# Attention of the small heads: score products by half row blocks, with ScalarE's order written out

## The chip, the core and the metric

The kernel runs on one core of one Trainium2 chip. The time is device microseconds (us) of one execution of the whole program, taken as the median of several runs. Five engines work beside each other, each through its own instructions in order: TensorE (PE in the profile; its weight loads are listed as PEld), VectorE (DVE), ScalarE (ACT), GpSimd (POOL) and SyncE (SP), which issues most of the DMA transfers. They wait for one another through semaphores. TensorE writes into PSUM, which has 8 banks; one bank holds 512 float32 numbers in each of 128 partitions.

## What is computed

The reference is a decoder of two layers over 16 sequences of 128 tokens with 256 features. Each layer has a self attention, a cross attention and a feed-forward part, each followed by a layer norm. The change is in the self attention of the second layer, which has 32 heads of 8 features each:

```python
def _sliding_window_attention(x, Wq, Wk, Wv, Wo, n_heads=32, window=128):
    B, T, D = x.shape                  # 16, 128, 256
    H, dk = (n_heads, D // n_heads)    # 32, 8
    bs = window
    nb = T // bs                       # 1
    ...
    scores = jnp.einsum('bhnrd,bhncd->bhnrc', qb, kw) * scale
    ...
    valid = (dist >= 0) & (dist <= window) & (key_global >= 0)
    scores = jnp.where(valid[None, None], scores, jnp.finfo(scores.dtype).min)
    probs = jax.nn.softmax(scores, axis=-1)
    out = jnp.einsum('bhnrc,bhncd->bhnrd', probs, vw)
    ...
    return out @ Wo.T
...
x = _layernorm(x + _L1_attn_ref(x, L1_attn_Wq, L1_attn_Wk, L1_attn_Wv, L1_attn_Wo), axis=-1)
```

With 128 tokens and a window of 128 each token attends to itself and to all tokens ahead of it in its own sequence, so that the mask is a plain causal one and every sequence stands alone.

## The kernel before

**The stages.** The program is one long body: the three parts of layer 0, then the self attention of layer 1 (the stage of the change, 1695 to 1963 us of the profile), the cross attention of layer 1 (to about 2198 us), and a mixture of experts. A planner decides the order of the instructions of each engine from costs of its own and from the order of the source. Inside `with tc.manual_schedule(engines={mybir.EngineType.PE})` TensorE's order is that of the source, and the planner orders the other engines around it.

**The unit of work.** The 2048 tokens are 16 row blocks of 128 tokens (`t`), one for each sequence. The 256 features of queries and keys, transposed, are two halves of 128 partitions (`c`), with 16 heads in each. Four neighbouring heads take up 32 partitions. `masked_keys` (L1230, on GpSimd) writes the keys four times side by side into `kz`, and in copy j keeps only the features of head j of each four, so that one product of 32 partitions of queries with 512 columns of `kz` gives the scores of four heads: 128 queries by 4 x 128 keys, one PSUM bank. A half (`t`, `c`) has four such products.

**A step** of the loop is (`t`, `c`, `e`): half a half, two products, eight heads. `attend_scores` does this for a step:

- TensorE writes the causal mask into two PSUM banks by two products with the identity in bf16 (L1238), and adds two score products (L1242) with 32 rows each, on two different row strips of its array. `sc` has two buffers of two banks.
- VectorE takes the maximum of each row and head (`amx`, L1251) and subtracts it (`pr`, L1253); ScalarE takes the exponent (L1254). `pr` has three buffers.

`attend_transpose` turns `pr` around by eight transposes (L1262), four into each of the two `tp` banks, and ScalarE copies each bank to `prT` (L1263). `attend_context` works on a half, that is on two steps: 16 products with the values and 16 with ones (L1272), four of them at a time on four column strips, which gives the weighted sums and the sums of the weights, in `o2`. `attend_divide` (L1282, L1284, VectorE) divides the one by the other and leaves `oT`. `attend_output` (L1301) multiplies both halves of a row block by the output weights, and VectorE adds the result to the residual `xs[t]` (L1302). `norm` (L110 to L116) is the layer norm of four row blocks, with a logarithm and an exponent on ScalarE (L102, L103); `norm_T` (L126, L127) transposes its result.

**The order of the source in a step n:** the scores of step n; the context of the half that ended at step n-3; the transposes of step n-2; and one further piece of work that depends on n: `project_a` (queries or keys of a later group of four row blocks, L1356 and L1360 on ScalarE, in row blocks 0 to 11), `values_a` (L1365, and L1367 on ScalarE), `norm_T`, or `attend_output` of the row block before. All of these share one PSUM bank, `misc`.

The PSUM banks of the stage: four for `sc`, two for `tp`, one for `misc`, one for `o2`.

The cross attention of layer 1 calls `attend_scores` too, with one product of 64 rows in each bank and no mask.

Of the kernel before, what the change touches and what calls it, by code (L numbers as in the profile page):

```python
# [18 lines left out]
F32 = mybir.dt.float32  # L19
# [8 lines left out]
P = 128  # L28
HID = 256
NB = 16  # L30
NT = NB * P
NG = 4
# [16 lines left out]
def decoder(ctx: ExitStack, tc: tile.TileContext, w: dict, out: bass.AP):  # L49
    nc = tc.nc  # L50
# [1179 lines left out]
        nc.gpsimd.tensor_tensor(kz, bc(kT, 1, 4), bc(own, 2, P), ALU.mult)  # L1230
        return kz

    def attend_scores(wk, psum, qT, kz, blocks, mask):

        sc = psum.tile([P, 2, 4, P], F32, tag="sc", name="sc", bufs=2)
        if mask is not None:
            for b in range(2):
                nc.tensor.matmul(  # L1238
                    sc[:, b].rearrange("p j k -> p (j k)"), lhsT=ident16, rhs=mask, start=True, stop=False
                )  # L1240
        for b, r in enumerate(blocks):
            nc.tensor.matmul(  # L1242
                sc[:, b].rearrange("p j k -> p (j k)"),
                lhsT=qT[r],
                rhs=kz[r].rearrange("p j k -> p (j k)"),
                start=mask is None,
                stop=True,
            )
        sc = sc.rearrange("p b j k -> p (b j) k")
        mx = stat.tile([P, 8], F32, tag="amx", name="amx")  # L1250
        nc.vector.tensor_reduce(mx, sc, AX.X, ALU.max)  # L1251
        pr = wk.tile([P, 8, P], F32, tag="pr", name="pr", bufs=3)
        nc.vector.tensor_tensor(pr, sc, bc(mx, 2, P), ALU.subtract)  # L1253
        nc.scalar.activation(pr, pr, AF.Exp)  # L1254
        return pr
# [69 lines left out]
    def cross_tables():  # L1325
        cross_w["own"] = own_rows(xpool, 64, "own2")
        cross_w["ones"] = places(xpool, D2, "ones2")

        gain = cross_w["rows"][0][1]
        nc.vector.tensor_scalar_mul(gain, gain, 0.25)  # L1330

    with ExitStack() as ph:
        pool = ph.enter_context(tc.tile_pool(name="l1a", bufs=1))
        wk = ph.enter_context(tc.tile_pool(name="l1a_k", bufs=2))
        ps = ph.enter_context(tc.tile_pool(name="l1a_ps", bufs=1, space=PSUM))
        D1 = 8
        wqk = [load_w(pool, f"L1_attn_{nm}T") for nm in ("Wq", "Wk")]
        wv = load_w(pool, "L1_attn_WvT")
        wz = attend_weights(pool, "L1_attn_WoT", D1)
        own1 = own_rows(pool, 32, "own1")  # L1340
        ones1 = places(pool, D1, "ones1")
        causal = pool.tile([P, 4, P], BF16, name="causal")
        nc.gpsimd.memset(causal, 0.0)
        nc.gpsimd.affine_select(
            out=causal, in_=causal, compare_op=ALU.is_ge, fill=NEG, base=0, pattern=[[0, 4], [-1, P]], channel_multiplier=1
        )
        o2 = ps.tile([P, 2, 2, P], F32, name="o2")
        cross_load()
        moe_load()
        vs, qkT = {}, {}  # L1350

        def project_a(g, n, c):

            pp = ps.tile([P, G], F32, tag="misc", name="proj")
            for k in range(2):
                nc.tensor.matmul(  # L1356
                    pp, lhsT=wqk[n][:, k, c * P : (c + 1) * P], rhs=xT[g][:, k, :], start=k == 0, stop=k == 1
                )
            t = qkT[g, n, c] = wk.tile([P, G], F32, tag=f"qkT{n}{c}", name=f"qkT{n}{c}")
            nc.scalar.activation(t, pp, AF.Copy, scale=1.0 / math.sqrt(D1) if n == 0 else 1.0)  # L1360

        def values_a(t):
            pp = ps.tile([P, HID], F32, tag="misc", name="proj_v")
            for k in range(2):
                nc.tensor.matmul(pp, lhsT=xTt(t, k), rhs=wv[:, k, :], start=k == 0, stop=k == 1)  # L1365
            v = wk.tile([P, HID], F32, tag="v", name="v")
            nc.scalar.copy(v, pp)  # L1367
            vs[t] = wk.tile([P, HID // D1, 4, D1], F32, tag="vz", name="vz", bufs=3)
            placed(v, ones1, D1, vs[t])

        steps = [(t, c, e) for t in range(NB) for c in range(2) for e in range(2)]
        kzs, prs, prTs, oTs = {}, {}, {}, {}
        with tc.manual_schedule(engines={mybir.EngineType.PE}):
            for n in range(2):
                for c in range(2):
                    project_a(0, n, c)
            values_a(0)
            for n in range(len(steps) + 16):
                if n == 4:
                    cross_tables()  # L1380

                if n in (5, 7):
                    q = NB // 2 - 2 + n // 7
                    norm_pair_xT(q, norm_pair_T(q, ps, "misc"))
                if n < len(steps):
                    t, c, e = steps[n]
                    cols = slice((t % 4) * P, (t % 4 + 1) * P)
                    if e == 0:
                        kzs[c] = masked_keys(wk, qkT[t // 4, 1, c][:, cols], own1)
                    blocks = [slice(32 * i, 32 * i + 32) for i in (2 * e, 2 * e + 1)]  # L1390
                    prs[n] = attend_scores(
                        wk, ps, qkT[t // 4, 0, c][:, cols], kzs[c], blocks, causal.rearrange("p j k -> p (j k)")
                    )
                if 0 <= n - 3 < len(steps):
                    t, c, e = steps[n - 3]
                    if e == 1:
                        attend_context([prTs.pop(n - 4), prTs.pop(n - 3)], vs[t], ones1, o2[:, c], 16 * c)
                        oTs[t, c] = attend_divide(wk, o2[:, c])
                if 0 <= n - 2 < len(steps):
                    prTs[n - 2] = attend_transpose(wk, ps, prs.pop(n - 2))  # L1400
                t, r = n // 4, n % 4
                if r == 0 and t // 4 + 1 < NG:
                    project_a(t // 4 + 1, t % 4 // 2, t % 2)
                elif r == 1 and t + 1 < NB:
                    values_a(t + 1)
                elif r == 3 and 0 <= t - 1 < NB:
                    attend_output(ps, t - 1, [oTs.pop((t - 1, c)) for c in range(2)], wz)
                    if t % 4 == 0:
                        norm(t // 4 - 1)
                elif r == 2 and t // 4 >= 1 and t % 4 in (1, 2):  # L1410
                    norm_T(t // 4 - 1, t % 4 - 1, ps, "misc")

# [1 line left out]
    with ExitStack() as ph:  # L1416
# [51 lines left out]
        with tc.manual_schedule(engines={mybir.EngineType.PE}):  # L1468
# [8 lines left out]
            for n in range(len(steps) + 14):  # L1477
                if n < len(steps):
                    t, c = steps[n]
                    if c == 0 and t + 2 < NB:  # L1480
                        load_ctx(t + 2)
                    blocks = [slice(64 * b, 64 * b + 64) for b in range(2)]
                    prs[n] = attend_scores(wk, ps, cols[t, 0][:, c, :], kzs.pop((t, c)), blocks, None)

                t, r = n // 2, n % 2
                if r == 0 and t + 2 < NB:
# [142 lines left out]
```

## Time and profile before

| | us |
|---|---|
| median of 3 runs | 2725.06 (2724.89 to 2730.54) |
| the profiled execution, its own time | 2732.66 |
| its span in the profile | 2730.9 |
| TensorE busy over the span | 2518.5 (92%) |
| VectorE busy over the span | 1902.3 (70%) |
| ScalarE busy over the span | 1473.7 (54%) |
| stage of the change, first score product to first score product of the next stage | 1695.48 to 1985.64 |

The page of the profile has the busy time of each engine; groups of instructions by source line with the mean time of one; and the chain of work that ended last. The trace can be asked for more: the busy times in a stretch, who waited for whom, and the timeline, in which each line has the start, the time taken, the engine, the source line, the operation, output <- inputs, the shapes, how many instructions the line merges (xN), and in brackets the idle time of the engine ahead of it with what ended it. A float32 product appears as two records (x2 for each), a transpose as one.

From the first score product of one row block to that of the next it took, for row blocks 0 to 14: 10.99, 19.05, 17.27, 17.28, 17.27, 17.71, 17.70, 17.28, 17.27, 17.71, 17.70, 17.28, 15.56, 15.99 and 15.99 us. Those of 17.70 hold a `norm_T`, those from row block 12 on hold no `project_a`.

### The profile page before, as it was taken

To read this page: it belongs to the slowest core of one execution; us is meant where nothing else is said; L and a number is where in the kernel's file an instruction comes from. 1 tells how busy PE (TensorE), PEld (TensorE's weight loads), DVE (VectorE), ACT (ScalarE), POOL (GpSimd) and SP (SyncE) were. 2 spreads that over 40 slices of the span, in tenths; PEclk is the share of its full clock that TensorE was granted. 3 is DMA by queue.
4 is the path that set the end of the run, shared out by engine and by line. 5 is a ranking of instruction groups with operands and counts; after the bars stand their busy time and mean duration, and the time that the engine had idled before them with its cause. 6 is when DMAs were issued, how large, how long until landed. Compare 5 with 4: busy or idle time off the path is not lost. (4 is left out here: it accounts for less than half of the span.)

```text
span 2730.9 us, 39531 instructions
## 1 busy us (share of the span) xinstructions
PE 2518.5 (92%) x13877; PEld 1493.5 (55%) x13908; DVE 1902.3 (70%) x4353; ACT 1473.7 (54%) x2778; POOL 1215.0 (44%) x1336
## 2 busy tenths in 40 slices
PE   6999999999986789988998888999988899999998
PEld 3677777777764133433433335666655546564746
DVE  5677777877757999999999963777777742324232
ACT  3455555555543888887887872555554531313120
POOL 5644544444436888888888873233132200000000
PEclk9999999999998899999999999999999999999999
DMA  7000000000011555655665562100100021111120
GB/s 226 1 1 1 1 1 1 1 1 1 1 50 29 106 116 111 128 122 107 119 125 110 113 136 97 55 2 2 42 16 11 2 63 47 54 39 60 34 67 10
DMA packets 360182, 150.82 MB, mean 55 GB/s; under 512 B 294576, under 2 KB 341136, under 8 KB 359472
## 3 DMA queue, kind: packets, MB, share of 16 engines
q1 hardware_dynamic: 358592, 144.49, 22.8%
q0 software_dynamic: 1392, 3.81, 0.6%
q8 instruction: 110, 1.80, 0.3%
q14 instruction: 88, 0.72, 0.1%
HBM read 74.71 MB, written 2.23 MB: 28 GB/s over the span
## 5 line engine op out<-in xcount | busy, mean ns | idle before, releaser
L786 POOL CAST aT<-at 128x2048 bf16<-128x2048 uint8 x256 | 480.9, 1894 | 91.5 <-DMA at<-a 88.6
L774 ACT ACTIVATE a<-e,snl 128x2048 uint8<-128x2048 f32 x256 | 510.7, 1996 | 3.5
L753 DVE TENSOR_SCALAR_CACHE_REDUCE e<-s,qs,smx 128x1024 f32<-128x1024 f32 x256 | 335.0, 1334 | 16.9 <-PE s L746 15.9
L753 DVE TENSOR_SCALAR_CACHE_REDUCE e<-s,qs 128x1024 f32<-128x1024 f32 x256 | 319.8, 1280 | 36.7 <-PE s L746 31.2
L796 PE MATMUL o<-aT,vq 128*32 128x512 bf16 x1024 | 262.8, 391 | 3.1 <-POOL aT L786 3.1
L746 PE MATMUL s<-kT,qT 64*128 64x512 bf16 x1024 | 191.0, 397 | 31.8 <-DVE e L753 28.7
L1541 DVE TENSOR_TENSOR h<-h,up 128x512 f32<-128x512 f32 (+1 forms) x100 | 68.7, 687 | 193.1 <-PE up L1537 189.4
L1540 ACT ACTIVATE h<-gate 128x512 f32<-128x512 f32 (+1 forms) x100 | 59.7, 597 | 220.1 <-PE gate L1537 219.9
L796 PEld LDWEIGHTS <-vq 128*32 128x32 bf16 x1024 | 85.5, 98 | 163.6 <-issue 89.4
L1537 PE MATMUL gate<-xT,w_L_ffn_w1g 128*128 128x512 f32 x352 | 167.7, 595 | 0.0
L1537 PE MATMUL up<-xT,w_L_ffn_w1u 128*128 128x512 f32 x352 | 165.4, 592 | 0.0
L1251 DVE TENSOR_REDUCE amx<-sc 128x8 f32<-128x1024 f32 x96 | 116.7, 1216 | 64.9 <-PE sc L1242 64.7
L1568 PE MATMUL py<-w_L_ffn_w2T,h 128*128 128x256 f32 x704 | 154.6, 379 | 0.0
L1254 ACT ACTIVATE pr<-pr 128x1024 f32<-128x1024 f32 x96 | 101.6, 1059 | 88.3 <-DVE pr L1253 88.3
L1263 ACT COPY prT<-tp 128x512 f32<-128x512 f32 x192 | 104.3, 584 | 76.7 <-PE tp L1262 76.3
L868 PE MATMUL gu<-xT,wgu 128*128 128x256 f32 x448 | 135.4, 427 | 9.2 <-ACT xT L160 4.3
L1568 PEld LDWEIGHTS py<-w_L_ffn_w2T,h 128*128 128x128 f32 x704 | 133.7, 190 | 18.3
L408 ACT ACTIVATE pls<-sc,lm,rms_rs 128x128 f32<-128x128 f32 x256 | 113.8, 454 | 21.6 <-DVE lm L404 21.6
L338 PE MATMUL proj<-Wlk,xT 128*128 128x512 f32 x256 | 121.1, 595 | 3.2 <-DVE ck L306 1.2
L338 PE MATMUL proj<-Wq,xT 128*128 128x512 f32 x256 | 122.0, 599 | 0.9 <-DVE raw_Wlk L347 0.9
L465 PE MATMUL po<-Wo,mT 128*128 128x256 f32 x512 | 121.2, 380 | 1.4 <-ACT mT L457 1.4
L1253 DVE TENSOR_TENSOR pr<-sc,amx 128x1024 f32<-128x1024 f32 x96 | 117.0, 1219 | 5.7
(313 smaller groups left out, 5378.9 us busy)
## 6 DMA issues: line engine op xcount, KB each, us to landing
wgu<-in_L_ffn_gu SPq DMA_DIRECT2D x112, 128.0 KB
sh<-share SPq DMA_DIRECT2D x32, 256.0 KB
at<-a SPq DMA_TRANSPOSE x256
sh<-share SPq DMA_DIRECT2D x16, 224.0 KB
sh<-share SPq DMA_DIRECT2D x16, 192.0 KB
w_L_ffn_w1g<-in_L_ffn_w1g SPq DMA_DIRECT2D x1, 2816.0 KB
w_L_ffn_w1u<-in_L_ffn_w1u SPq DMA_DIRECT2D x1, 2816.0 KB
w_L_ffn_w2T<-in_L_ffn_w2T SPq DMA_DIRECT2D x1, 2816.0 KB
```

The source lines that it names most:

```text
L338: nc.tensor.matmul(pp.rearrange("p h d -> p (h d)"), lhsT=xTt(b, k), rhs=wts[nm, hg][:, k, :], start=k == 0, stop=k == 1)
L465: nc.tensor.matmul(outs[b], lhsT=st["mT"][:, h, :], rhs=wts["Wo", hg][:, h, :], start=hg == 0 and h == 0, stop=hg == 3 and h == 3,)
L746: nc.tensor.matmul(s[hh][:, c, :], lhsT=qT[t % 4][r, i, :], rhs=kT[r, i, at : at + G], start=True, stop=True)
L753: nc.vector.tensor_scalar(st["e"][hh][:, half, :], s[hh].rearrange("p a b -> p (a b)"), qs[2 * gp + u][:, 2 * i + hh : 2 * i + hh + 1], No ...
L774: nc.scalar.activation(a.bitcast(U8), st["e"][hh].rearrange("p a b -> p (a b)"), AF.Exp, bias=st["nm"][:, hh : hh + 1], accum_out=groups[g ...
L786: nc.gpsimd.tensor_copy(aT[:, :, hh, u * P : (u + 1) * P].rearrange("p (b j) q -> p b j q", j=2), st["at"][hh].bitcast(U8).rearrange("p b ...
L796: nc.tensor.matmul(o[r : r + 32].rearrange("p a b -> p (a b)"), lhsT=vq[:, n, 32 * i : 32 * i + 32], rhs=aT[:, n].rearrange("p a b -> p (a ...
L868: nc.tensor.matmul(ffn_ps[q][:, n, :], lhsT=wt[:, k, :], rhs=xT[q // 2][:, k, at], start=k == 0, stop=k == 1)
L1251: nc.vector.tensor_reduce(mx, sc, AX.X, ALU.max)
L1253: nc.vector.tensor_tensor(pr, sc, bc(mx, 2, P), ALU.subtract)
L1537: nc.tensor.matmul(pp[:rows], lhsT=wt[:, k, :], rhs=xT[g][:, k, :], start=k == 0, stop=k == 1)
L1568: nc.tensor.matmul(py, lhsT=h[:rows, i4 * P : (i4 + 1) * P], rhs=wt, start=n == 0, stop=n == len(parts) - 1)
```

## The change

The loop goes by halves (`t`, `c`) in place of steps. `attend_scores` now takes four row strips and both `sc` buffers at once: four mask products, then four score products on the four row strips, each into its own bank. What VectorE and ScalarE do with the scores is split off as `attend_exp`. `pr` has four buffers here and three in the cross attention, where nothing else changes.

The source order in a half h is: scores of half h; `project_a` or `norm_T`, if any; the context and division of half h-2; then for each of the two quarters e: maximum, subtraction and exponent of (h, e), and the transposes with their copies of (h-1, e); then `values_a`, or `attend_output` of the row block before and perhaps `norm`. ScalarE is now in the `manual_schedule` too, so that its instructions stand in this order: exponent of (h, 0), the two copies of (h-1, 0), exponent of (h, 1), the two copies of (h-1, 1). VectorE's and GpSimd's order is still the planner's.

```diff
@@ -1230,26 +1230,24 @@
         nc.gpsimd.tensor_tensor(kz, bc(kT, 1, 4), bc(own, 2, P), ALU.mult)
         return kz
 
-    def attend_scores(wk, psum, qT, kz, blocks, mask):
-
-        sc = psum.tile([P, 2, 4, P], F32, tag="sc", name="sc", bufs=2)
+    def attend_scores(psum, qT, kz, blocks, mask):
+
+        scs = [psum.tile([P, 2, 4, P], F32, tag="sc", name="sc", bufs=2) for _ in range(len(blocks) // 2)]
+        banks = [sc[:, b].rearrange("p j k -> p (j k)") for sc in scs for b in range(2)]
         if mask is not None:
-            for b in range(2):
-                nc.tensor.matmul(
-                    sc[:, b].rearrange("p j k -> p (j k)"), lhsT=ident16, rhs=mask, start=True, stop=False
-                )
-        for b, r in enumerate(blocks):
+            for bank in banks:
+                nc.tensor.matmul(bank, lhsT=ident16, rhs=mask, start=True, stop=False)
+        for bank, r in zip(banks, blocks):
             nc.tensor.matmul(
-                sc[:, b].rearrange("p j k -> p (j k)"),
-                lhsT=qT[r],
-                rhs=kz[r].rearrange("p j k -> p (j k)"),
-                start=mask is None,
-                stop=True,
+                bank, lhsT=qT[r], rhs=kz[r].rearrange("p j k -> p (j k)"), start=mask is None, stop=True
             )
-        sc = sc.rearrange("p b j k -> p (b j) k")
+        return [sc.rearrange("p b j k -> p (b j) k") for sc in scs]
+
+    def attend_exp(wk, sc, bufs):
+
         mx = stat.tile([P, 8], F32, tag="amx", name="amx")
         nc.vector.tensor_reduce(mx, sc, AX.X, ALU.max)
-        pr = wk.tile([P, 8, P], F32, tag="pr", name="pr", bufs=3)
+        pr = wk.tile([P, 8, P], F32, tag="pr", name="pr", bufs=bufs)
         nc.vector.tensor_tensor(pr, sc, bc(mx, 2, P), ALU.subtract)
         nc.scalar.activation(pr, pr, AF.Exp)
         return pr
@@ -1368,47 +1366,56 @@
             vs[t] = wk.tile([P, HID // D1, 4, D1], F32, tag="vz", name="vz", bufs=3)
             placed(v, ones1, D1, vs[t])
 
-        steps = [(t, c, e) for t in range(NB) for c in range(2) for e in range(2)]
-        kzs, prs, prTs, oTs = {}, {}, {}, {}
-        with tc.manual_schedule(engines={mybir.EngineType.PE}):
+
+
+
+        halves = [(t, c) for t in range(NB) for c in range(2)]
+        prs, prTs, oTs = {}, {}, {}
+
+        def transposed(h, e):
+            if 0 <= h < len(halves):
+                prTs[h, e] = attend_transpose(wk, ps, prs.pop((h, e)))
+
+        with tc.manual_schedule(engines={mybir.EngineType.PE, mybir.EngineType.Activation}):
             for n in range(2):
                 for c in range(2):
                     project_a(0, n, c)
             values_a(0)
-            for n in range(len(steps) + 16):
-                if n == 4:
+            for h in range(len(halves) + 8):
+                t, c = h // 2, h % 2
+                if h == 2:
                     cross_tables()
-
-                if n in (5, 7):
-                    q = NB // 2 - 2 + n // 7
+                if h < len(halves):
+                    cols = slice((t % 4) * P, (t % 4 + 1) * P)
+                    scs = attend_scores(
+                        ps,
+                        qkT[t // 4, 0, c][:, cols],
+                        masked_keys(wk, qkT[t // 4, 1, c][:, cols], own1),
+                        [slice(32 * i, 32 * i + 32) for i in range(4)],
+                        causal.rearrange("p j k -> p (j k)"),
+                    )
+
+                if c == 0 and t // 4 + 1 < NG:
+                    project_a(t // 4 + 1, t % 4 // 2, t % 2)
+                elif c == 1 and t // 4 >= 1 and t % 4 in (1, 2):
+                    norm_T(t // 4 - 1, t % 4 - 1, ps, "misc")
+                elif h in (3, 5):
+                    q = NB // 2 - 2 + h // 4
                     norm_pair_xT(q, norm_pair_T(q, ps, "misc"))
-                if n < len(steps):
-                    t, c, e = steps[n]
-                    cols = slice((t % 4) * P, (t % 4 + 1) * P)
-                    if e == 0:
-                        kzs[c] = masked_keys(wk, qkT[t // 4, 1, c][:, cols], own1)
-                    blocks = [slice(32 * i, 32 * i + 32) for i in (2 * e, 2 * e + 1)]
-                    prs[n] = attend_scores(
-                        wk, ps, qkT[t // 4, 0, c][:, cols], kzs[c], blocks, causal.rearrange("p j k -> p (j k)")
-                    )
-                if 0 <= n - 3 < len(steps):
-                    t, c, e = steps[n - 3]
-                    if e == 1:
-                        attend_context([prTs.pop(n - 4), prTs.pop(n - 3)], vs[t], ones1, o2[:, c], 16 * c)
-                        oTs[t, c] = attend_divide(wk, o2[:, c])
-                if 0 <= n - 2 < len(steps):
-                    prTs[n - 2] = attend_transpose(wk, ps, prs.pop(n - 2))
-                t, r = n // 4, n % 4
-                if r == 0 and t // 4 + 1 < NG:
-                    project_a(t // 4 + 1, t % 4 // 2, t % 2)
-                elif r == 1 and t + 1 < NB:
+                if 0 <= h - 2 < len(halves):
+                    u, d = halves[h - 2]
+                    attend_context([prTs.pop((h - 2, e)) for e in range(2)], vs[u], ones1, o2[:, d], 16 * d)
+                    oTs[u, d] = attend_divide(wk, o2[:, d])
+                for e in range(2):
+                    if h < len(halves):
+                        prs[h, e] = attend_exp(wk, scs[e], 4)
+                    transposed(h - 1, e)
+                if c == 0 and t + 1 < NB:
                     values_a(t + 1)
-                elif r == 3 and 0 <= t - 1 < NB:
-                    attend_output(ps, t - 1, [oTs.pop((t - 1, c)) for c in range(2)], wz)
+                elif c == 1 and 0 <= t - 1 < NB:
+                    attend_output(ps, t - 1, [oTs.pop((t - 1, d)) for d in range(2)], wz)
                     if t % 4 == 0:
                         norm(t // 4 - 1)
-                elif r == 2 and t // 4 >= 1 and t % 4 in (1, 2):
-                    norm_T(t // 4 - 1, t % 4 - 1, ps, "misc")
 
 
 
@@ -1480,7 +1487,8 @@
                     if c == 0 and t + 2 < NB:
                         load_ctx(t + 2)
                     blocks = [slice(64 * b, 64 * b + 64) for b in range(2)]
-                    prs[n] = attend_scores(wk, ps, cols[t, 0][:, c, :], kzs.pop((t, c)), blocks, None)
+                    (sc,) = attend_scores(ps, cols[t, 0][:, c, :], kzs.pop((t, c)), blocks, None)
+                    prs[n] = attend_exp(wk, sc, 3)
 
                 t, r = n // 2, n % 2
                 if r == 0 and t + 2 < NB:
```

## The prediction

> **What bounds the kernel now.** I read the busy times of the stage first, then TensorE's idle time by group, then the timeline of one row block. Busy times of the stretch that holds the stage (us, then busy time and records of PE, PEld, DVE, ACT, POOL, the granted clock, DMA's share and rate):
>
> ```profile
> 1695.00:1963.00 268.00, 263.72 (x3014) 166.48 (x3047) 206.73 (x244) 148.15 (x230) 77.35 (x59) 1.00 0.08 29
> ```
>
> TensorE is busy for 264 of 268 us at the full clock, VectorE for 207, DMA hardly at all. Two groups of TensorE between 1725.5 and 1963 us (busy, mean ns | idle ahead):
>
> ```profile
> L1242 PE MATMUL sc<-kz,qkT 32*128 32x512 f32 x224 | 63.1, 640 | 2.6
> ...
> L1262 PE MATMUL tp<-ident,pr 128*128 128x128 f32 x448 | 61.2, 280 | 0.0
> ```
>
> The transposes, which need ScalarE's exponents and empty `tp` banks, find both there always. TensorE waits for nobody; its order and the prices of its instructions set the pace. The timeline gives the prices:
>
> ```profile
> 1822.25 1.13 PE L1242 MATMUL sc<-kz,qkT 32*128 32x512 f32 x4
> 1822.43 2.38 POOL L1226 TENSOR_TENSOR vz<-v,ones 128x1024 f32<-128x1024 f32 x1 [1.11 <-ACT v L1367]
> 1822.63 1.06 ACT L1254 ACTIVATE pr<-pr 128x1024 f32<-128x1024 f32 x1 [0.28 <-DVE pr L1253]
> 1823.31 0.81 PEld L1272 LDWEIGHTS o<-prT,vz 128*32 128x32 f32 x32 [0.76 <-DVE pr L1253]
> 1823.31 1.08 PE L1272 MATMUL o<-prT,vz 128*32 128x128 f32 x32
> 1823.42 1.22 DVE L1251 TENSOR_REDUCE amx<-sc 128x8 f32<-128x1024 f32 x1 [0.83 <-PE sc L1242]
> ...
> 1824.75 1.22 DVE L1253 TENSOR_TENSOR pr<-sc,amx 128x1024 f32<-128x1024 f32 x1
> ...
> 1825.19 1.09 PE L1262 MATMUL tp<-ident,pr 128*128 128x128 f32 x8
> 1825.89 0.95 DVE L1282 RECIPROCAL ors<-o 128x128 f32<-128x128 f32 x1
> 1826.01 1.06 ACT L1254 ACTIVATE pr<-pr 128x1024 f32<-128x1024 f32 x1 [2.32 <-DVE pr L1253]
> ...
> 1826.87 0.29 DVE L1284 TENSOR_TENSOR oT<-o,ors 128x128 f32<-128x128 f32 x1
> 1826.97 1.06 ACT L1263 COPY prT<-tp 128x512 f32<-128x512 f32 x2
> ...
> 1828.63 1.03 PE L1301 MATMUL py<-z_L_attn_WoT,oT 128*128 128x256 f32 x4
> ...
> 1829.50 0.59 PE L1238 MATMUL sc<-causal,ident 128*128 128x512 bf16 x2
> ...
> 1830.03 1.13 PE L1242 MATMUL sc<-kz,qkT 32*128 32x512 f32 x4
> ```
>
> Prices on TensorE from start to start: two masks 0.53 (1829.50 to 1830.03), a pair of scores 1.06 (1822.25 to 1823.31), a context 1.88 (to 1825.19), the transposes of a step 0.93 (1825.19 to the next mask at 1826.12), `py` 0.87 (1828.63 to 1829.50), values 0.86, `project_a` 1.73 (1816.62 to 1818.35). One row block: 4 x (0.53 + 1.06) + 2 x 1.88 + 4 x 0.93 + 1.73 + 0.86 + 0.87 = 17.30. Measured: 17.27 and 17.28. The account closes without a wait.
>
> **What TensorE saves.** A second mask adds 0.21 (0.59 for two against 0.38 for one), so four cost 0.53 + 2 x 0.21 = 0.95. Scores: the two products on two row strips start 0.007 us apart in the trace's records, so a pair costs what one does. No row has four row strips; the nearest is the context, where four column strips run together (32 records of 0.107 in 0.90, not 3.4). Bounds: 1.06 for four if they run as two do, 2 x 0.96 = 1.9 if they run pair after pair. I take 1.06. A half is then 0.95 + 1.06 = 2.01 in place of 3.18: 2.34 a row block, 37 us in 16. TensorE's own work is 14.96 a block.
>
> [...]
>
> **What it adds: two waits in each half.** I follow the order of each engine in the changed program from a half's first score product (0). VectorE's distances: scores to `amx` 1.17 (1822.25 to 1823.42), `amx` to `pr` 1.33, `pr` to the next 1.14, reciprocal to `oT` 0.98. The changed program keeps VectorE's order `amx`, `pr`, `amx`, `pr`, reciprocal, `oT`. So `amx` 1.17, `pr` 2.50, `amx` 3.64, `pr` 4.97, reciprocal 6.11, `oT` 7.09 to 7.38. ScalarE starts the exponent of (h, 0) at 2.50 + 1.22 + 0.03 = 3.75, and the next instruction 0.96 later (1826.01 to 1826.97).
>
> *First wait.* Transposes of (h-1, 0) fill both `tp` banks; those of (h-1, 1) need them emptied, and the two copies now stand behind the exponent of (h, 0). Behind the waiting transposes stand everything else on TensorE, first the values or `py`.
>
> *Second wait.* `py` of row block t-1 needs `oT` of its second half, whose context ran in this very half. In the kernel before it ran a step earlier. Here `oT` is VectorE's last item, at 7.38. The next half's masks stand behind `py`.
>
> What TensorE needs after a wait (signal and weight load) no row shows, as it never waits here; I take 0.15, between 0.05 (signals of other engines: 0.03 to 0.05) and 0.25.
>
> Second half of a block (c = 1): context 1.06 to 2.94, transposes to 3.87. Copies: 3.75 + 0.96 = 4.71, done 5.29 and, 0.47 later, 5.76. TensorE goes on at 5.44, waits again for the second bank (5.91), done 6.38; first product of `py` to 6.81; the second waits for `oT` until 7.53, to 7.96; four masks: 8.91. Without waits it would be 6.62.
>
> First half (c = 0): `project_a` to 2.79, context to 4.67, transposes to 5.60. First bank full and copied from 5.37 (0.70 after the start of the transposes, as at 1827.70 to 1828.40), done 5.95 and 6.42. TensorE goes on at 6.10, second bank 6.57, done 7.04, values 7.90, masks 8.85.
>
> Sum: 17.76 a block against 17.28: **+0.48**. The wait eats the 2.34 and a little more. A `norm_T` (0.44) now hides in the first wait of c = 1.
>
> By stretches, against the measured row blocks:
> - Start. The first scores come 0.43 later (two more masks). Half 0 to half 1: masks 3 and 4 wait for `pr` of (0, 1), done at 6.19, so 6.86. Half 1 has no context, its transposes end at 6.38, masks 7.33. Block 0: 14.19 against 10.99, +3.2. Block 1: 17.76 against 19.05, -1.3. Together +2.3.
> - Blocks 2, 3, 4, 7, 8, 11: 6 x 0.48 = +2.9.
> - Blocks 6 and 10 (`norm_T`, 17.70): +0.1.
> - Blocks 5 and 9: after `py` VectorE has the residual, the statistics, a wait for ScalarE's logarithm and exponent, and four normalisations (0.41 each), all ahead of `amx`: 7.96 + 0.45 + 0.46 + 0.20 + 0.65 + 4 x 0.41 = 11.4 against 8.91 + 1.17 = 10.1. Of the 1.3, 0.65 stays, as `project_a` fills the rest: 18.4 against 17.7, 2 x 0.7 = +1.4.
> - Blocks 12 to 14, without `project_a`: c = 0 goes as c = 1 to 6.38, values 7.24, masks 8.19; 17.10 a block. Against 15.56 and 15.99: +1.5 and +1.1, and block 13 has the whole 1.3 of the norm: +2.4. Together +5.1.
> - Block 15 to the next stage: both drain; I take 0, between -1.5 and +1.5.
>
> Sum +11.8. The profiled span of 2730.9 becomes 2742.7; the median is 5.8 below that span, so 2725.06 + 11.8 = **2737**.
>
> **Costed at nothing.** GpSimd: `kz` and `vz` keep their order, 2 x 1.04 + 2.38 = 4.5 in 17 us, and `kz` of a half needs only queries projected long before; if it were late, the scores would be late by as much. SyncE's queue keeps its order. A fourth `pr` buffer removes no wait. The cross attention's own work is unchanged and starts later by the sum. A norm's logarithm on ScalarE, now in fixed order, has the next exponent behind it, and is in the 0.65.
>
> **Rivals.**
> 1. *TensorE stays the bound* (faster). If copies and `oT` are there when TensorE comes, a block is 14.96 and the time falls by up to 37 us: 2688. It decides from a chain under 8.64 a half (17.28 / 2), against my 8.85 and 8.91; over the whole stage the chain must be 0.37 (11.8 / 32) shorter a half to be even. For it: only 0.2 are missing in the middle blocks. Against: each link is a measured distance, and orders on TensorE, ScalarE and VectorE are fixed. A likely such case, 0.8 shorter a half: 2737 - 26 = 2711. Chance 0.08.
> 2. *The same mechanism, 0.2 to 0.5 shorter a half*, from restarts of 0.05 and a better drain: 3 restarts x 0.1 x 32 = 9.6 less, so 2727, no change. Chance 0.10.
> 3. *Four products run as two pairs*. The change then does not do what it says. The second pair ends 0.86 later; 32 x 0.86 = 27 if all of it is on the chain. The first pair is free for VectorE on time, which hides most: I take a third, 9 us, 2746, at most 2764. Restarts of 0.25 (+9.6) give as much. For it: no row shows four. Against: the context's four column strips. Chance 0.17.
>
> **How the numbers follow.** My forecast, 2731 to 2746, has 0.65. The range is 2729 to 2752: below it lie rival 1 and half of rival 2 (0.13), above it the far part of rival 3 (0.06). No change is 0.2%, 5.5 us, about what a measurement can tell: 2719.6 to 2730.5. Faster 0.08, same 0.10, slower 0.82.
>
> **What would show it.** In the changed profile: transposes (tp) idle for `prT` of ScalarE, about 0.5 in c = 0 and 1.5 in c = 1; `py` idle for `oT` about 0.7; row blocks of 17.8 in the middle, 17.1 to 18.4 at the end; TensorE's busy time in the stage down by some 37 us or its share well under 98%; four score products within 0.03 us of each other. Wrong, if TensorE has no such idle time, or if the scores take 1.9.

## The result, and the profile after

| | before | after |
|---|---|---|
| median | 2725.01 us (2724.89 to 2730.54, 4 runs) | 2748.59 us (2747.68 to 2749.90, 4 runs) |
| the profiled execution, its own time | 2732.66 | 2749.90 |
| its span | 2730.9 | 2748.0 |
| first score product of the stage to that of the next stage | 290.16 | 309.72 |
| from there to the end | 745.26 | 745.37 |

The changed kernel is slower: 1.0076 times the time before, interval 1.0061 to 1.0090. The whole loss is in the stage of the change, +19.56 us; what follows takes as long as before. Of the 23.6 us between the medians the other 4 are of the size by which executions of one and the same kernel differ (below).

The row blocks, first score product to first score product, in us; the last column is row block 15 to the next stage:

| block | 0 | 1 | 2, 3, 4, 7, 8, 11 | 6, 10 | 5, 9 | 12 | 13 | 14 | 15 |
|---|---|---|---|---|---|---|---|---|---|
| before | 10.99 | 19.05 | 17.28 | 17.70 | 17.71 | 15.56 | 15.99 | 15.99 | 38.11 |
| predicted | 14.19 | 17.76 | 17.76 | 17.76 | 18.4 | 17.10 | 18.4 | 17.10 | 38.1 |
| after | 15.04 | 18.37 | 17.98 | 17.98 | 18.77 | 17.07 | 21.40 | 17.07 | 39.35 |

Busy times of row blocks 2 to 11, before and then after (us, then busy time and records of PE, PEld, DVE, ACT, POOL, the granted clock, DMA's share and rate):

```profile
1725.50:1900.00 174.50, 172.51 (x1959) 108.72 (x1978) 131.72 (x159) 95.11 (x148) 49.99 (x38) 1.00 0.01 2
```

```profile
1726.30:1907.80 181.50, 160.82 (x1964) 102.76 (x1983) 133.84 (x159) 93.53 (x149) 49.56 (x38) 1.00 0.01 2
```

TensorE, busy for 172.5 of 174.5 us before, is now busy for 160.8 of 181.5, both at the full clock: there is less for it to do and it takes longer. The transposes' group before is shown in the prediction, without idle time; `py` had none either. The groups say where TensorE stands idle (busy, mean ns | idle ahead <- what ended it), first `py` before (1725.5 to 1963 us), then three groups after (1725 to 1963 us):

```profile
L1301 PE MATMUL py<-z_L_attn_WoT,oT 128*128 128x256 f32 x56 | 14.4, 380 | 0.0
```

```profile
L1260 PE MATMUL tp<-ident,pr 128*128 128x128 f32 x416 | 59.0, 286 | 23.1 <-ACT prT L1261 23.1
L1241 PE MATMUL sc<-kz,qkT 32*128 32x512 f32 x208 | 29.8, 642 | 0.0
...
L1299 PE MATMUL py<-z_L_attn_WoT,oT 128*128 128x256 f32 x54 | 17.5, 407 | 6.9 <-DVE oT L1282 6.9
```

The score products keep the mean time of one, 642 ns against 640, but their group is busy for 29.8 us (208 records) instead of 63.1 (224): four run at a time in place of two. Two groups that had waited for nothing wait for 30 us, the transposes for ScalarE's copies of the `tp` banks, `py` for VectorE's `oT`. The timeline of one row block has each of these waits in its place:

```profile
1817.08 1.14 PE L1241 MATMUL sc<-kz,qkT 32*128 32x512 f32 x8
1818.15 1.98 PE L1354 MATMUL proj<-xT,w_L_attn_WkT 128*128 128x512 f32 x4
...
1820.06 1.08 PE L1270 MATMUL o<-prT,vz 128*32 128x128 f32 x32
...
1821.94 1.09 PE L1260 MATMUL tp<-ident,pr 128*128 128x128 f32 x8
...
1823.33 1.15 PE L1260 MATMUL tp<-ident,pr 128*128 128x128 f32 x8 [0.29 <-ACT prT L1261]
...
1826.14 1.14 PE L1241 MATMUL sc<-kz,qkT 32*128 32x512 f32 x8
...
1829.90 1.06 ACT L1252 ACTIVATE pr<-pr 128x1024 f32<-128x1024 f32 x1 [3.94 <-DVE pr L1251]
1830.86 1.05 ACT L1261 COPY prT<-tp 128x512 f32<-128x512 f32 x2
...
1831.48 1.14 PE L1260 MATMUL tp<-ident,pr 128*128 128x128 f32 x8 [1.30 <-ACT prT L1261]
...
1832.46 0.60 PE L1299 MATMUL py<-z_L_attn_WoT,oT 128*128 128x256 f32 x2
1833.22 0.29 DVE L1282 TENSOR_TENSOR oT<-o,ors 128x128 f32<-128x128 f32 x1
...
1833.57 0.70 PE L1299 MATMUL py<-z_L_attn_WoT,oT 128*128 128x256 f32 x2 [0.51 <-DVE oT L1282]
...
1835.06 1.14 PE L1241 MATMUL sc<-kz,qkT 32*128 32x512 f32 x8
```

Eight records of the scores are four products; with 1.14 us they take what two took before (1.13). Second half of the block (from 1826.14): ScalarE sat idle for 3.94 us until VectorE had `pr`, takes the exponent at 1829.90 and only then the copies, at 1830.86; the second transposes wait 1.30 us for the first of the two. `py` needs `oT`, which starts at 1833.22 as VectorE's last work of the half, and waits another 0.51. In the first half the transposes wait 0.29. That is 2.10 us of shown idle time in 17.98.

Block 13 is longer than blocks 12 and 14 by 4.3 us. Its lines of the timeline, and the busy times of the stretches around them:

```profile
1925.80 2.23 DVE L116 TENSOR_SCALAR x<-x,ln_mv,ln_rstd 128x256 f32<-128x256 f32 x4 [0.60 <-ACT ln_rstd L103]
...
1932.04 1.97 PE L1260 MATMUL tp<-ident,pr 128*128 128x128 f32 x8 [3.14 <-ACT prT L1261]
```

```profile
1924.00:1932.00 8.00, 4.85 (x84) 3.06 (x82) 7.16 (x11) 2.22 (x6) 1.04 (x1) 0.93 0.01 2
1932.00:1934.00 2.00, 1.96 (x9) 1.96 (x10) 1.97 (x3) 1.63 (x3) 0.00 (x0) 0.50 0.00 0
1934.00:1938.00 4.00, 3.78 (x12) 1.85 (x15) 0.00 (x1) 1.24 (x3) 1.74 (x1) 0.55 0.00 0
1938.00:1942.00 4.00, 4.00 (x84) 2.97 (x76) 3.31 (x3) 1.42 (x2) 1.66 (x2) 1.00 0.00 0
```

The norm's four normalisations stand ahead of the maxima on VectorE, all of the half's chain comes later, and TensorE stands still for 3.14 us. Then its granted clock is 0.50: the eight transposes take 1.97 us instead of 1.14, and the clock is back at 1.00 only from 1938 on. The same happens once at the start of the stage, after a gap of 3.10 us at 1701.8 (0.50 from 1705.5 to 1708.9). In the profile before, the clock was full from 1688.4 to 1971.6 us, which takes in row blocks 0 to 14.

### The profile page after: what moved, and what is told of

The parts are those of the page before. It is cut to its first block, busy times and chain, and to the rows that moved or that the text cites. A ratio compares the mean times of both kernels' runs of the same rounds, so it can differ in the third digit from the quotient of the medians.

```text
span 2748.0 us, 39573 instructions
## 1 busy us (share of the span) xinstructions
PE 2496.8 (91%) x13877; PEld 1483.8 (54%) x13908; DVE 1904.6 (69%) x4353; ACT 1469.7 (53%) x2778; POOL 1215.3 (44%) x1336
## 3 DMA queue, kind: packets, MB, share of 16 engines
HBM read 74.71 MB, written 2.23 MB: 28 GB/s over the span
## 5 line engine op out<-in xcount | busy, mean ns | idle before, releaser
L1226 POOL TENSOR_TENSOR vz<-v,ones 128x1024 f32<-128x1024 f32 (+1 forms) x32 | 58.6, 1830 | 175.6 <-ACT v L1365 90.4
L1260 PE MATMUL tp<-ident,pr 128*128 128x128 f32 x768 | 107.7, 284 | 30.0 <-ACT prT L1261 30.0
```

What stands on the lines that cost most here:

```text
L1260: nc.tensor.transpose(pt[:, j, :], pr[:, 4 * b + j, :], ident)
```

## The experiments

Theory A in all of them is that of the prediction: four strips do save TensorE its 2.3 us a block, and the two new waits, behind VectorE's chain, take them back; from the trace after it also has the lowered clock (0.50) after the long gaps (3.10 and 3.14 us). The rivals differ and stand in the expectations. All stage times are, as above, from the first score product to that of the next stage, from the one profile of each run.

### The kernel before, once more (e0_before)

No edit.

> The kernel before, profiled once more. The two profiles differ by 17.1 us in span (2730.9 and 2748.0), the medians by 23.6. Theory A: the profiled execution of before was a slow one (2732.66 against a median of 2725.0); a new profile has a span near 2723 to 2725, and shows where the other 6 us lie; outside of the changed stage, which takes 290.2 us from its first score product to the next stage's (1695.48 to 1985.64) in both. Theory B: the stage itself varies; then its 290.2 us become some 284, and the change costs 23 us in the stage.

Measured: 2732.00 us (10 runs) beside 2730.28 (25 runs), ratio 1.0004 (0.9987 to 1.0020). Stage 290.37, against 290.16 in the first profile; row blocks as before. So this stage repeats within 0.2 us, which is against Theory B; the new span of 2729.3 us is not the 2723 to 2725 of Theory A either, and runs of this one kernel went from 2721.50 to 2737.82. What varies lies ahead of the stage: over the profiles of all kernels here its first score product came between 1684.6 and 1699.0 us, while the work after the stage took 745 to 748. Effects of the order are therefore read below from the stage, and the ratios say whether they reach the total.

### The changed kernel, once more (a2_after)

No edit.

> The changed kernel once more, beside the kernel before on the same chip. The stage took 290.2 and 290.4 us in two profiles of before and 309.7 in the one of after; what lies ahead of it varied by 4 us from run to run. Theory A (the change costs what the stage shows): 19 to 21 us over before, a ratio of 1.0068 to 1.0077. Theory B (the first medians, 23.6 apart, are right): 1.0085 or more, which needs another cost outside of the stage.

Measured: 2746.83 us beside 2727.17, ratio 1.0068 (1.0049 to 1.0088), +19.7 us; stage 307.56. This is Theory A. The middle blocks are the same 17.98; block 13 took 20.08 instead of 21.40, with a shorter stretch of lowered clock (3.4 us instead of 6.8) after the same 3.14 us gap. The size of that effect differed between the two profiles; the middle blocks did not.

### One wait away: copies ahead of the exponent (e1_copies_first)

```diff
                 for e in range(2):
+                    transposed(h - 1, e)
                     if h < len(halves):
                         prs[h, e] = attend_exp(wk, scs[e], 4)
-                    transposed(h - 1, e)
```

> The changed kernel with one edit: the transposes and copies of (h-1, e) stand ahead of the exponent of (h, e), so the copies no longer stand behind the exponent. Theory A (both waits stand, in series with VectorE): the first wait falls from about 1.5 to 0.4 in the second halves (0.4 remains, since two tp banks are emptied 1.3 us after the transposes start and TensorE is through with them after 0.9), but the wait for oT grows by as much, so the row blocks of the middle stay within 0.3 of 17.98; the row blocks without project_a fall by about 1 each, and the two gaps of over 3 us on TensorE are gone, and with them the half clock after them (about 3 us): 2738 to 2744. Rival (the exponent ahead of the copies is the whole cost): a row block falls by 1.3 or more, 2725 or less.

Measured: 2739.74 us, ratio 1.0036 (1.0021 to 1.0052); stage 301.82; middle blocks 17.98, to the hundredth what they were. TensorE's groups in the same stretch:

```profile
L1260 PE MATMUL tp<-ident,pr 128*128 128x128 f32 x448 | 62.7, 283 | 7.9 <-ACT prT L1261 7.9
...
L1239 PE MATMUL sc<-causal,ident 128*128 128x512 bf16 x81 | 24.2, 379 | 4.0 <-DVE pr L1251 2.7
L1299 PE MATMUL py<-z_L_attn_WoT,oT 128*128 128x256 f32 x54 | 17.2, 403 | 14.4 <-DVE oT L1282 14.4
```

The transposes' wait shrinks from 23.1 to 7.9 us and that of `py` grows from 6.9 to 14.4. The timeline has these waits in one middle block:

```profile
1816.05 1.15 PE L1260 MATMUL tp<-ident,pr 128*128 128x128 f32 x8 [0.29 <-ACT prT L1261]
...
1823.20 1.14 PE L1260 MATMUL tp<-ident,pr 128*128 128x128 f32 x8 [0.30 <-ACT prT L1261]
...
1826.29 0.70 PE L1299 MATMUL py<-z_L_attn_WoT,oT 128*128 128x256 f32 x2 [1.51 <-DVE oT L1282]
```

That is 0.29 + 0.30 + 1.51 = 2.10 us in place of 0.29 + 1.30 + 0.51 = 2.10. A wait removed ahead of another that ends later on the same chain only makes that one longer. What was gained, 7.9 us of stage, comes from elsewhere: the norm blocks (17.8 instead of 18.8), row blocks 12 and 14 (16.07 instead of 17.07) and block 13 (18.48). That the half clock would go with the long gaps was a miss: in block 13 a gap of 2.18 us is left and the clock still falls to 0.50 between 1926 and 1928.

### The other wait away: `py` a row block later (e2_output_later)

```diff
-                elif c == 1 and 0 <= t - 1 < NB:
-                    attend_output(ps, t - 1, [oTs.pop((t - 1, d)) for d in range(2)], wz)
-                    if t % 4 == 0:
+                elif c == 1 and 0 <= t - 2 < NB:
+                    attend_output(ps, t - 2, [oTs.pop((t - 2, d)) for d in range(2)], wz)
+                    if t % 4 == 1:
                         norm(t // 4 - 1)
```

(`norm_T` moves by one row block with it.)

> The changed kernel with one edit: attend_output comes one row block later, when its oT has long been there (the norm and norm_T follow it by as much). Theory A: the wait for oT is gone, the wait for the copies stays; the second half falls by 0.6 to 0.8, a row block to 17.2 to 17.4; sum 16 x 0.7 = 11: 2735 to 2740. Rival: the wait for oT hides behind the first; no change, 2746 to 2750.

Measured: 2730.14 us, ratio 1.0002 (0.9989 to 1.0016); stage 293.30; middle blocks 17.21, blocks 12 and 13 16.30. The groups:

```profile
L1260 PE MATMUL tp<-ident,pr 128*128 128x128 f32 x452 | 63.3, 283 | 23.1 <-ACT prT L1261 23.1
...
L1299 PE MATMUL py<-z_L_attn_WoT,oT 128*128 128x256 f32 x56 | 14.4, 380 | 0.0
```

`py` waits no more, the transposes as long as before, and the blocks lose 0.77. The stage gained 16.4 us where 11 had been expected (2735 to 2740 us in all), because the norm now falls into block 14, which has 17.22 with it, after a gap of 2.29 us that no lowered clock follows (1.00 from 1937.2 to 1941.2 us); block 13 is at 16.30 instead of 21.40. At the start a gap of 3.11 us with the lowered clock (a mean of 0.72 over 1706 to 1710 us) is still there. This one edit brings the kernel back to the time before.

### Both (e3_both)

The two edits together.

> Both edits together. Theory A: with neither wait in the way, TensorE's own work of 14.96 a row block, 0.4 twice for the tp banks and VectorE's round for the scores (6.9 a half) are what is left: 16.0 to 16.8 a row block in the middle, about 14.2 at the end, less than before (17.28, 15.6 to 16.0): 2710 to 2719. Rival (four row strips do not save what the sum says, or another wait takes over): not under 2725.

Measured: 2717.29 us, ratio 0.9952 (0.9935 to 0.9970); stage 279.98; middle blocks 16.21 (16.7 to 16.8 with a `norm_T`), 14.29 in blocks 12 and 13. Together they save 1.77 a block where the one alone saved nothing and the other 0.77: two waits in series. What is left of the two waits is that for the first copy, 0.29 twice a block in the timeline.

### Both waits gone: transposes on both sides of the context (e7_spread)

```diff
+                transposed(h - 1, 0)
                 if 0 <= h - 2 < len(halves):
                     u, d = halves[h - 2]
                     attend_context(...)
                     oTs[u, d] = attend_divide(wk, o2[:, d])
                 for e in range(2):
+                    if e == 1:
+                        transposed(h - 1, 1)
                     if h < len(halves):
                         prs[h, e] = attend_exp(wk, scs[e], 4)
-                    transposed(h - 1, e)
```

with the later `py` of e2_output_later. The context (1.88 us) now lies between the transposes that fill the `tp` banks and those that need them empty.

> The changed kernel with attend_output one row block later and the transposes taken apart: those of (h-1, 0) right after project_a, then the context, then those of (h-1, 1), with ScalarE's order kept as copies (h-1, 0), exponent (h, 0), copies (h-1, 1), exponent (h, 1). The context (1.88) now stands between the two sets of transposes and hides the 0.4 that the two tp banks cost. Theory A (waits were all that ate the gain): first halves 8.4, second halves 6.9 (VectorE's round for the scores), a row block 15.2 to 15.8; the stage from its first score product to the next stage's falls from 290.3 to 264 to 272, the time to 2703 to 2714. Rival (another bound, e.g. VectorE at 7.4 a half, comes first): a row block stays over 16.2 as with both single edits (stage 280.0), 2716 or more.

Measured: 2706.27 us beside 2728.49, ratio 0.9917 (0.9898 to 0.9936): faster than both kernels. Stage 266.29, middle blocks 15.26 (15.7 and 16.1 with a `norm_T` or norm). The groups:

```profile
L1260 PE MATMUL tp<-ident,pr 128*128 128x128 f32 x464 | 62.4, 277 | 0.0
...
L1299 PE MATMUL py<-z_L_attn_WoT,oT 128*128 128x256 f32 x64 | 16.7, 383 | 0.6 <-DVE x L1300 0.6
```

Neither group waits for a copy or for `oT`. In row blocks 3 to 5 TensorE stands idle for nothing at all:

```profile
1740.00:1785.70 45.70, 45.70 (x589) 30.75 (x588) 37.85 (x45) 26.49 (x43) 14.20 (x10) 1.00 0.01 2
```

TensorE's own work in a block is 15.26 by this run; the prediction had 14.96. Elsewhere some 3 us are left at the masks, which wait for VectorE's `pr`, 1.80 of them in block 14, which holds a norm.

### The same without the later `py` (e8_spread_py_now)

> As e7_spread, but attend_output stays in the half in which its oT is made. Theory A (the wait for oT alone costs what the two single edits together hid): TensorE waits for oT about 1.7 in each second half; a row block of 17.3 to 17.5, the stage 291 to 296. Rival (the spread transposes alone bring the gain): under 16.5.

Measured: 2743.53 us in one run, stage 297.29, 31.0 more than e7_spread; middle blocks 17.42, but 18.22 and 18.26 in blocks 7 and 8. The groups:

```profile
L1260 PE MATMUL tp<-ident,pr 128*128 128x128 f32 x440 | 59.6, 279 | 0.0
...
L1299 PE MATMUL py<-z_L_attn_WoT,oT 128*128 128x256 f32 x56 | 18.1, 406 | 23.0 <-DVE oT L1282 23.0
```

The whole wait is now on `py`: 1.93 us in row blocks 3 and 4, 1.49 in blocks 2, 6 and 10, where TensorE has more work of its own, and the block takes 17.42 either way. With no wait at the transposes at all, the wait for `oT` alone costs 2.16 a block. The stage is a little above what was expected, since the clock fell to 0.50 after four of the seven gaps of 1.92 or 1.93 us (last section); one such stretch lies across blocks 7 and 8.

### Four strips or two pairs, in the changed order (e5_pairs) and in the one without waits (e9_spread_pairs)

```diff
-        if mask is not None:
-            for bank in banks:
-                nc.tensor.matmul(bank, lhsT=ident16, rhs=mask, start=True, stop=False)
-        for bank, r in zip(banks, blocks):
+        for n in range(0, len(banks), 2):
+            if mask is not None:
+                for bank in banks[n : n + 2]:
+                    nc.tensor.matmul(bank, lhsT=ident16, rhs=mask, start=True, stop=False)
+            for bank, r in zip(banks[n : n + 2], blocks[n : n + 2]):
```

> The changed kernel with one part undone: the scores pair by pair (two masks, two products, twice), loop and orders as changed. Theory A (in the changed order the waits eat most of what four strips save): TensorE has 1.1 a half more to do and waits the less; a row block of 18.5 to 19.1 against 17.98, where the same edit cost 2.26 in the order without waits (17.52 against 15.26); the stage 308 to 314. Rival: the full 2.2, row blocks of 20.

> As e7_spread, but with the scores pair by pair: two masks, two products, two masks, two products, so only two row strips at once. Theory A (four row strips run in the time of two): against e7_spread each half has 0.22 more for the masks' switch and 1.06 for the scores, 32 x 1.1 = 35 at most, less where VectorE's round is the longer one: the stage 286 to 298, a row block 17.1 to 18.0. Rival (four strips give little): within 8 us of e7_spread's stage.

Measured, one run each: e5_pairs 2757.14 us, stage 313.13, middle blocks 18.70. e9_spread_pairs 2738.95, stage 293.48, middle blocks 17.52. So the same part of the change is worth 18.70 - 17.98 = 0.72 a block in the order that the change chose, and 17.52 - 15.26 = 2.26 in the order without waits. Over the stage it is 27.2 us in the order without waits and 3.4 in the other (5.6 with the changed kernel's second profile); those last two hold the price of the clock that fell in blocks 0 and 13 of the changed kernel, while in e5_pairs it stayed full (1.00) through block 14. The row blocks compare the waits alone. TensorE's group of the scores in e5_pairs shows two at a time again, and its waits are small:

```profile
L1242 PE MATMUL sc<-kz,qkT 32*128 32x512 f32 x208 | 58.6, 640 | 0.0
L1261 PE MATMUL tp<-ident,pr 128*128 128x128 f32 x408 | 57.1, 283 | 8.2 <-ACT prT L1262 8.2
```

The order alone, with pairs, is no gain either: 293.48 in e9_spread_pairs, whose transposes and `py` wait for nothing, against 290.16 before.

### ScalarE's order left to the planner (e4_act_free)

```diff
-        with tc.manual_schedule(engines={mybir.EngineType.PE, mybir.EngineType.Activation}):
+        with tc.manual_schedule(engines={mybir.EngineType.PE}):
```

> The changed kernel with ScalarE's order left to the planner, as before. In its order the copies of (h-1, 0) stand behind both exponents of half h in every first half. Theory A (the wait for the copies depends on ScalarE's order): the first wait grows by an exponent and VectorE's 2.5, a row block becomes 19.2 to 20.2, the stage 322 to 335, the time 2758 to 2775. Rival (ScalarE's order does not matter, since VectorE's round sets the pace): a row block of 18.0, as in the changed kernel.

Measured: 2773.97 us in one run, stage 341.22, row blocks 1 to 11 at 19.5 to 23.7: 31.5 us of stage worse than the changed kernel, and more than was expected of the stage. In the timeline ScalarE takes both exponents of a half (here at 1831.48 and 1833.94) before the copies:

```profile
1833.94 1.06 ACT L1252 ACTIVATE pr<-pr 128x1024 f32<-128x1024 f32 x1 [0.92 <-DVE pr L1251]
...
1834.90 1.06 ACT L1261 COPY prT<-tp 128x512 f32<-128x512 f32 x2
...
1835.52 1.97 PE L1260 MATMUL tp<-ident,pr 128*128 128x128 f32 x8 [1.84 <-ACT prT L1261]
```

The wait is longer, and 1.97 for the eight transposes is again the lowered clock (a mean of 0.69 over 1834 to 1838 us); the longest waits here are 3.6 us, and the clock fell ten times in row blocks 0 to 13, which is part of the 31.5 us. So writing ScalarE's order out is what kept the change from losing a further 31.5 us; it was not what made it slow.

### The long gaps filled with work that nobody reads (e10_filler)

```diff
                     transposed(h - 1, e)
+                    if e == 0 and h in (1, 26):
+                        warm = ps.tile([P, G], F32, tag="misc", name="warm")
+                        for _ in range(5):
+                            nc.tensor.matmul(
+                                warm, lhsT=ident16, rhs=causal.rearrange("p j k -> p (j k)"), start=True, stop=True
+                            )
```

Five products more on TensorE at the start of each of the two long gaps; no wait is removed.

> The changed kernel with more work: five products of the identity with the mask, which nothing reads, between the two sets of transposes of halves 1 and 26, where TensorE stands still for 3.1 us (at 1701.8 and 1928.9) and the granted clock falls to 0.50 after it. Theory A (the gap brings the clock down): row block 13 falls from 21.40 to 18.4 to 19.0 and row block 0 from 15.04 to 14.1 to 14.4, the stage from 309.7 to 306 or less, though TensorE has 2.2 us more to do. Rival (row block 13 is long because VectorE's four normalisations took 2.23 and TensorE's order waits): 21.4 or more.

Measured: 2738.91 us in one run, stage 307.06, above the 306 expected. The gap in block 13 is 2.06 us instead of 3.14, and the clock stays full after it:

```profile
1923.66 1.15 PE L1260 MATMUL tp<-ident,pr 128*128 128x128 f32 x8 [2.06 <-ACT prT L1261]
```

```profile
1923.70:1925.70 2.00, 2.00 (x13) 1.65 (x14) 1.89 (x3) 1.63 (x3) 0.00 (x0) 1.00 0.00 0
1925.70:1927.70 2.00, 2.00 (x13) 0.67 (x12) 0.05 (x1) 1.06 (x3) 0.86 (x1) 1.00 0.00 0
```

The block takes 18.78, what blocks 5 and 9 take, instead of 21.40 (20.08 in the second run). Only the products differ, so the lowered clock is worth 2.6 there (1.3 in the second run), and the norm's own lateness 1.7 (18.78 against the 17.07 of blocks 12 and 14). At the start it is a miss: the clock still fell to 0.50 between 1698.0 and 1701.4, row block 0 got shorter (14.28) and row block 1 longer (19.09).

## Why the prediction was right, and what it had too small

Right in direction and cause. The stage lost 19.6 us where 11.4 had been worked out for it (the 11.8 of the prediction counts 0.43 ahead of the first score product). The time was less well placed than the cause: 2748.59 us lies above the forecast of 2731 to 2746, in the part of the range that was kept for rival 3, two pairs, and rival 3 did not happen. That the range held it is luck. By its own steps:

**What TensorE saves: right.** Four score products on four strips cost 1.07 (1826.14 to 1827.21) where 1.06 had been taken, and not the 1.9 of the upper bound. Rival 3, two pairs, fell with that. In the order without waits the saving is 2.26 a block by e9_spread_pairs, predicted 2.34. The transposes' wait of 23.1 us in the changed kernel is one for banks to be emptied. It was a matter of order and not of the copies' speed: in e7_spread the same copies, with the same four strips, hold nothing up (0.0). TensorE's busy time in the stage fell from 281.0 to 264.1 us, 17 and not the 37 that the prediction gave as a sign; the share of the stage, 97 to 85%, shows what the sign was meant to show.

**The second half of a block: right almost to the hundredth.** From the first score product, predicted and measured: exponent 3.75 and 3.76, copies 4.71 and 4.72, transposes go on 5.44 and 5.34, `oT` 7.09 and 7.08, second half of `py` 7.53 and 7.43, next scores 8.91 and 8.92. The restart price of 0.15 was divided otherwise: 0.04 to 0.06 lie between the end of the work waited for and the first product, and the group behind it takes 0.05 (transposes) to 0.10 (`py`) longer than in a row without waits. The sum held.

**The first half: too small by 0.2.** 9.06 instead of 8.85, and nearly all of it is one term: `project_a` was priced at 1.73 from the kernel before, where it follows transposes. After score products it costs 1.91 (1818.15 to 1820.06); its mean record is 618 ns in every kernel here that has it right behind the scores, against 593 before. Ten blocks with some 0.2 each are 2.0 of the 2.5 that blocks 2 to 11 lost beyond the forecast (+6.9 instead of +4.4); the rest is in blocks 5 and 9, where the normalisations took 2.23 us instead of the 4 x 0.41 = 1.64 of the prediction.

**Two waits in series: right, and the centre of it.** e1_copies_first shows it best: in the middle blocks one wait is away, and the other takes it over whole. Rivals 1 and 2, that the chain is shorter than it looks, fell: 9.06 and 8.92 us a half against the 8.85 and 8.91 predicted.

**Row blocks 12 to 14: right but for the clock.** Blocks 12 and 14 were predicted at 17.10 and took 17.07. Block 13 was predicted at 18.4 by the norm's 1.3, and without the lowered clock it is 18.78. Its normalisations, too, took 2.23 instead of 1.64, on the same path, which would cover the other 0.4; they ran beside a `kz` of GpSimd, which the prediction had costed at nothing (last section). With the clock it is 21.40. This is the term that was left out: the prediction worked out that everything in block 13 comes late, priced the lateness, and put at nothing the granted clock of 0.50 that came with the gap of 3.14 us and lasted 6.8. In row blocks 0 to 14 its trace had no gap to show it. In block 15, whose change it took as 0, the trace had one, 2.28 us long, with the clock at 0.50 behind it:

```profile
1972.62 1.45 PE L126 MATMUL ln_pt<-ident,x 128*128 128x128 f32 x4 [2.28 <-DVE x L116]
```

```profile
1974.00:1978.00 4.00, 2.65 (x9) 1.92 (x9) 0.00 (x0) 1.17 (x2) 2.71 (x4) 0.50 1.09 359
```

**The start: +3.4 instead of +1.9** in row blocks 0 and 1. Here too the clock was at 0.50, from 1705.5 to 1708.9, after a gap of 3.10. The filler did not remove it, so its price there is argued, not shown. As an estimate: in block 13 of the second run a stretch of the same 3.4 us cost 1.3, and with that much taken off, +3.4 would be +2.1, near the +1.9.

**Row block 15 to the next stage: +1.24**, predicted 0 within 1.5; 0.45 in the second run. Its cause stays open.

The rest between 19.6 and the 23.6 of the medians is the spread of what runs ahead of the stage; the second, longer comparison had 19.7.

## What to carry to other kernels

Work that is taken off the engine that sets the pace is gained only as far as the order behind it lets the engine run: the same four strips were worth 0.72 us a row block in one order and 2.26 in another, and the difference was where two consumers (a bank to be copied out, a quotient of the same half) stood. Before such a change write down when each thing that the shortened engine needs next is ready, on every engine, and put a piece of its own work between filling a bank and needing it empty; judge waits in series together, as removing the first alone can show nothing in the loop. Count also what a stop can cost after it ends: in block 13 the lowered clock was worth 2.6 us in one profile of the changed kernel and 1.3 in the other.

## What the runs showed of the hardware

**Gaps of TensorE and its granted clock.** All eight gaps of 3.10 to 3.61 us in the stage (two in each profile of the changed kernel, one in e2_output_later, three in e4_act_free) came with a granted clock of 0.50, for 3.4 to 6.8 us, which began at the earliest 1.5 us before the end of the gap and at the latest 1.4 us after it. Of the 41 gaps of 1.79 to 2.29 us in the stages of all 13 profiles 30 did (it fell in the gap or at most 2.2 us after it), among them the one of 2.28 us in block 15 that every profile has, before and after; of the 73 gaps of 1.0 to 1.53 us none did. In e8_spread_py_now seven blocks had the same gap of 1.92 or 1.93 us, and the clock fell after four. Stretches of 2 us behind one that was not followed and one that was:

```profile
1764.60:1766.60 2.00, 2.00 (x10) 0.98 (x14) 1.03 (x3) 0.00 (x0) 0.00 (x0) 1.00 0.00 0
...
1905.40:1907.40 2.00, 2.00 (x10) 0.85 (x14) 1.03 (x3) 0.00 (x0) 0.00 (x0) 0.76 0.00 0
1907.40:1909.40 2.00, 2.00 (x9) 0.50 (x10) 0.07 (x1) 0.00 (x0) 0.00 (x0) 0.50 0.00 0
```

After a gap of 2.18 in e1_copies_first it fell, after one of 2.29 in e2_output_later it did not. In block 13 the stretch at 0.50 was 6.8 and 3.4 us long in the changed kernel's two profiles, after the same gap of 3.14, and at the start of e10_filler 3.4. Why equal gaps differ no run shows.

**Normalisations beside GpSimd's keys.** The four of the norm in block 13 took 2.23 us in both profiles of the changed kernel and in e10_filler, where the `kz` of GpSimd (1.04 us) began 0.4 us after them; 1.38 before, in e2_output_later (block 14) and in e7_spread, where none did. It is so without exception for the norms in the stages of all 13 profiles: 17 groups with `kz` beside them took 2.23, 35 without it 1.37 or 1.38, and e8_spread_py_now has both (2.23 in blocks 5 and 9, 1.38 in block 13). Where it is 2.23, the second of the four takes 1.25 to 1.26 us instead of 0.41 and the others do not. Whether the one holds up the other was not tried by itself and is not shown.
